# A two-layer feed-forward stage whose TensorE and ScalarE instructions are put in the program's order

## The chip, the cores and the metric

The kernel runs on one core of one Trainium2 chip, as one launch. The metric is the device time of that launch in microseconds (us). TensorE is called PE in the profile (its weight loads PEld), VectorE DVE, ScalarE ACT, GpSimd POOL; SP only issues DMAs.

## The reference

Eight sublayers run one after another on 2048 tokens of width 128. The change is in the sixth, "L2 feed-forward" (`l2f`), which is itself two layers of local attention followed by a gated MLP. Cut to what matters:

```python
def _layer(x, wqkv, qs, ksc, wo, lg, lb, w1, b1, w2, b2):
    h = shift_token(x)                       # half of the channels from the token before
    q, k, v = split(h @ wqkv)                # 8 heads of 64
    q = l2norm(q) * qs ; k = l2norm(k) * ksc
    q, k = rotary_xpos(q, k)
    o = local_attention(q, k, v)             # window 64: own window and the one before
    x = x + o @ wo
    h = layernorm(shift_token(x)) * lg + lb
    a, g = split(h @ w1 + b1)                # 341 + 341
    return x + (a * gelu(g)) @ w2 + b2
```

After the two layers, `l2f` adds its own input and normalizes again. All of it is float32.

## The kernel before, in words

`l2f` works on tiles of 128 tokens (16 a layer, so T = 32 tiles in all) and on blocks of four tiles (512 tokens, four a layer). A software pipeline runs over **ticks**; at one tick several functions run, each for another tile. For tile t:

- `project(t)`, at tick t: two matmuls of 512 columns give q and k into a PSUM tile `p`; ScalarE squares it into `sq` (L1095), VectorE sums the squares per head into `rn` (L1099), multiplies `p` by the rotary tables into `qk` (L1108) and, in two halves, into the reused `sq` (L1110, L1111), and GpSimd adds the two (L1113). At each odd tick ScalarE takes the root of `rn` for two tiles (L1102), GpSimd clips it (L1103), VectorE inverts it (L1104), and GpSimd scales `qk` of both tiles (L1118). A third matmul gives v, which ScalarE copies out (L1122).
- `turn(t)`, at tick t+2: eight transposes of `qk`, then ScalarE copies `qT` (L1139) and `kT` (L1140), and GpSimd takes the 64 columns before from the last `kT` (L1144).
- `probs(t)`, at tick t+3: two bf16 matmuls add the mask (L1153, the "band"), 32 small ones the scores (L1165) into the PSUM tile `s`; VectorE takes the maxima `em` (L1173), ScalarE makes eight exponentials (L1178), VectorE inverts the sums `den` (L1185) and GpSimd scales `e` (L1186).
- `turn_probs(t)`, at tick t+4: eight transposes of `e` (L1194), which VectorE copies to `et` (L1196).
- `mixed(t)`, at tick t+4: 32 small matmuls of `et` with v into `po` (L1211); ScalarE copies `po` into the block's `oT` (L1218).
- `ff1` to `ff7`, for a whole block, one a tick: output projection and residual; shift and layer norm; the transposes back; the first MLP matrix with gelu (`ff4`: three pairs of matmuls in `p2` tiles, L1263, gelu L1266, product L1269); the second matrix (`ff5`); the last norm (`ff6`, `ff7`, second layer only). `forward(tick, odd)` calls those that are due. Piece k is due when `tick - 8 - k` is a multiple of four.

So four ticks make a period. I call them by their piece: **A** (tick a multiple of 4: `ff1`, and `ff5` of the block before), **B** (`ff2`, and `ff6` in the second layer), **C** (`ff3`, `ff7`), **D** (`ff4`).

[...] The pool `p2` holds three tiles of two banks, shared in turn by `s`, `p`, the transposes of `turn` and `turn_probs`, and the three accumulators of `ff4`. The pool `ps_t` holds two tiles of one bank (`tp`), shared by v's product, `po`, and every accumulator and transpose of the pieces except `ff4`'s.

The order in which an engine takes its instructions is set when the program is built: a scheduler takes what it reckons ready first, by priorities that follow the program, and picks the buffer of each tile. Each engine then works through its own list in that order, and waits on semaphores. The order of the tick's calls is

```python
for tick in range(T + 11):
    due = lambda lag: 0 <= tick - lag < T
    forward(tick, True)      # ff5, ff6, ff7
    if due(3): probs(tick - 3)
    if due(0): project(tick)
    forward(tick, False)     # ff1 .. ff4
    if due(4): turn_probs(tick - 4)
    if due(2): turn(tick - 2)
    if due(4): mixed(tick - 4)
```

The activation tables of Sqrt, Exp and Gelu are loaded separately (ACT_TABLE_LOAD in the profile).

## Time and profile before

| | |
|---|---|
| runs | 2861.51, 2861.67, 2853.43 us; median 2861.51 |
| profiled execution | 2845.6 us, span 2843.8 us |
| mean granted TensorE clock | 0.949 |
| busy, share of the span | PE 90%, PEld 57%, DVE 58%, ACT 52%, POOL 22% |
| `l2f`, first projection to the first matmul of the next stage | 824.07 to 1273.13 us |

The median of the runs is 15.9 us (0.56%) above the profiled execution, and the runs lie within 8.2 us of each other. Windows below are microseconds from the start of the span.

### The profile page before, as it was taken

What the parts mean: (1) busy time and instruction counts of PE and PEld (TensorE: products, weight loads), DVE (VectorE), ACT (ScalarE), POOL (GpSimd) and SP (SyncE); (2) the same over time, 40 slices, a digit from 0 to 9 for tenths busy, and PEclk for the clock granted to TensorE, in tenths of its full rate; (3) what the DMA queues carried; (4) which work ended last, traced back from release to release, by engine and by line L of the source; (5) the groups of instructions that cost most, each with busy time, mean ns of one, the idle gap of its engine ahead of it and who ended that gap; (6) DMA issues with size and microseconds to landing.
All of it is one profiled execution on the core that took longest, in us unless ns stands there. A gap on an engine that the chain in (4) does not pass through costs nothing.

```text
span 2843.8 us, 59514 instructions
## 1 busy us (share of the span) xinstructions
PE 2564.7 (90%) x24826; PEld 1608.3 (57%) x24826; DVE 1650.6 (58%) x2624; ACT 1474.9 (52%) x2968; POOL 632.4 (22%) x773
## 2 busy tenths in 40 slices
PE   5789569988878888879999999999999999999998
PEld 3456334432225444436777767777677776777543
DVE  6443242116676566546777767777677776777411
ACT  1113212234537666536676666666567665766422
POOL 2142341015568666520000000000000000000000
PEclk9679868989989999989999999999999999999999
DMA  3101100000011111010000000000000000000000
GB/s 142 56 22 37 32 13 6 0 23 8 8 51 40 27 31 53 19 41 13 10 6 9 9 6 9 9 6 9 9 6 9 9 6 9 6 9 6 1 8 8
DMA packets 30930, 55.59 MB, mean 20 GB/s; under 512 B 5388, under 2 KB 18644, under 8 KB 29380
## 3 DMA queue, kind: packets, MB, share of 16 engines
q1 hardware_dynamic: 27958, 45.09, 5.5%
q0 software_dynamic: 2272, 4.66, 0.7%
q8 instruction: 198, 3.24, 0.5%
q10 hardware_dynamic: 432, 2.04, 0.2%
q14 instruction: 70, 0.57, 0.1%
HBM read 29.49 MB, written 4.71 MB: 12 GB/s over the span
## 4 chain that ended last, share of the span: by engine, by line
PE 77%; DVE 12%; POOL 4%; ACT 3%; issue 2%; DMA 1%; SPq 0%; POOLq 0%; DVEq 0%; ACTq 0%
PE po L1438 17%; PE s L1399 16%; PE t L1423 10%; PE mm L834 8%; PE h L645 2%; DVE h L980 2%; PE tp L675 1%; PE tp L1476 1%; PE tp L1379 1%; PE p L1087 1%; PE p L1263 1%; PE mm L823 1%; PE tp L1501 1%; DVE ln_xn L276 1%; PE mm L845 1%
## 5 line engine op out<-in xcount | busy, mean ns | idle before, releaser
L1413 ACT ACTIVATE e<-s,nm 128x1024 f32<-128x1024 f32 x512 | 574.2, 1121 | 395.5 <-DVE nm L1407 395.5
L1407 DVE TENSOR_REDUCE nm<-s 128x1 f32<-128x1024 f32 x512 | 602.6, 1219 | 40.4 <-PE s L1399 40.2
L1438 PE MATMUL po<-et,v 128*64 128x128 f32 x8192 | 505.6, 276 | 0.0
L1399 PE MATMUL s<-kT,qT 64*128 64x512 f32 x1024 | 495.0, 603 | 1.2 <-ACT e L1413 1.2
L1399 PE MATMUL s<-kT,qx 64*128 64x512 f32 x1024 | 494.9, 603 | 0.0
L1425 DVE COPY et<-t 128x512 f32<-128x512 f32 x512 | 350.8, 685 | 211.0 <-ACT et L1426 93.0
L1438 PEld LDWEIGHTS po<-et,v 128*64 128x64 f32 x8192 | 443.5, 137 | 17.5 <-issue 0.2
L1423 PEld LDWEIGHTS t<-con,e 64*128 64x128 f32 x8192 | 319.8, 139 | 207.8 <-issue 109.1
L1423 PE MATMUL t<-con,e 64*128 64x64 f32 x8192 | 358.0, 226 | 2.9 <-ACT e L1413 1.7
L1426 ACT COPY et<-t 128x512 f32<-128x512 f32 x512 | 301.3, 588 | 49.3 <-PE t L1423 49.1
L1457 POOL TENSOR_TENSOR f<-m,nm 128x8 f32<-128x8 f32 x64 | 12.9, 202 | 1117.9 <-DVE m L1455 1117.9
L834 PE MATMUL mm<-h,w 128*128 128x512 f32 x512 | 221.1, 592 | 0.1
L1399 PEld LDWEIGHTS s<-kT,qT 64*128 64x128 f32 x1024 | 173.3, 189 | 62.4 <-issue 51.8
L1399 PEld LDWEIGHTS s<-kT,qx 64*128 64x128 f32 x1024 | 173.3, 188 | 59.3 <-ACT e L1413 31.1
L834 PEld LDWEIGHTS mm<-h,w 128*128 128x128 f32 x512 | 97.2, 190 | 122.3 <-issue 119.4
L847 DVE SCALAR_TENSOR_TENSOR r<-mm,vec,xT 128x512 f32<-128x512 f32 x8 | 6.0, 751 | 239.8 <-PE mm L845 239.8
L841 ACT ACTIVATE h<-mm,vec 128x512 f32<-128x512 f32 x64 | 44.0, 687 | 157.3 <-PE mm L834 157.2
L1178 ACT ACTIVATE e<-p,em 128x128 f32<-128x128 f32 x256 | 90.5, 381 | 40.6 <-DVE em L1173 38.6
L272 POOL TENSOR_SCALAR ln_rs<-ln_mv 128x4 f32<-128x4 f32 x40 | 10.5, 264 | 425.3 <-DVE ln_mv L270 387.2
L1413 ACT ACTIVATION_READ_ACCUMULATOR e<-s,nm 128x1 f32 x512 | 102.7, 201 | 0.0
L284 PE MATMUL tp<-con,ln_xn 128*128 128x128 f32 x144 | 33.0, 336 | 64.2 <-DVE ln_xn L276 64.2
L986 POOL TENSOR_TENSOR hc<-h,bc 128x1024 f32<-128x1024 f32 x32 | 75.2, 2351 | 63.9 <-DVE h L980 53.9
(340 smaller groups left out, 3782.1 us busy)
## 6 DMA issues: line engine op xcount, KB each, us to landing
qx<-qT SPq DMA_DIRECT2D x64, 128.0 KB, 2.2
vo<-v SPq DMA_DIRECT2D x62, 128.0 KB, 2.2
ex<-in_w_ex_dram SPq DMA_DIRECT2D x4, 1536.0 KB, 14.2
rot<-in_rot_dram SPq DMA_DIRECT2D x32, 128.0 KB, 2.3
w<-in_w_l2f_dram SPq DMA_DIRECT2D x2, 1557.0 KB
w<-in_w_l1f_dram SPq DMA_DIRECT2D x1, 2816.0 KB, 9.7
w<-in_w_l3f_dram SPq DMA_DIRECT2D x1, 2816.0 KB
yd<-ys SPq DMA_DIRECT2D x39, 64.0 KB, 1.5
```

Of the source, the lines that this page charges most:

```text
L645: nc.tensor.matmul(h[:, i], lhsT=xt, rhs=self.ex[:, bass.ds(e, 1), i * 512 : (i + 1) * 512].rearrange("p a b -> p (a b)"), start=False, st ...
L834: nc.tensor.matmul(p, lhsT=hid[i][:, k, c * 128 : (c + 1) * 128], rhs=h[:, k, :], start=k == 0, stop=k == 3,)
L980: nc.vector.tensor_tensor_scan(h[:, i], dA[:, i], pu[:, i], carry_of[b - 1][:, g : g + 1], ALU.mult, ALU.add)
L986: nc.gpsimd.tensor_mul(hc, h, bc[:, 1].unsqueeze(1).to_broadcast([128, 2, TB]))
L1178: nc.scalar.activation(e[:, r, c, :], s[:, r, c, :], AF.Exp, bias=m[:, r, c : c + 1], accum_out=den[:, r, c : c + 1],)
L1399: nc.tensor.matmul(p[:, i, :], lhsT=q_of[b, 4 * g + h][i][r, t * 128 : (t + 1) * 128], rhs=kT[r, g, c * 512 : (c + 1) * 512], start=True, ...
L1407: nc.vector.tensor_reduce(nm_of[k][:, h, c : c + 1], p, AX.X, ALU.max, negate=True)
L1413: nc.scalar.activation(e, p, AF.Exp, bias=nm_of[k][:, h, c : c + 1], accum_out=den_of[k][:, h, c : c + 1])
L1423: nc.tensor.transpose(tp[i][:, j, :], e[r, j * 128 : (j + 1) * 128], self.ident[r, r])
L1425: nc.vector.tensor_copy(et[:, 0], tp[0])
L1426: nc.scalar.copy(et[:, 1], tp[1])
L1438: nc.tensor.matmul(po_of[k][r, h, :].rearrange("p (i q) -> p i q", i=2), lhsT=v[:, t, g * 64 : (g + 1) * 64], rhs=ets[c][:, :, j, :], star ...
```

## The change

It is in `l2f` alone. (1) A `manual_schedule` block over PE and Activation makes those two engines take their instructions in the order in which the program states them; VectorE, GpSimd and SP stay with the scheduler. (2) `mixed` runs at tick t+5 in place of t+4, between `project` and the pieces. (3) The root and what follows it leave `project` and become `norms`, called at the end of each odd tick behind the pieces. (4) All pieces run at one place, behind `mixed`, in reversed order (`ff7` first). (5) VectorE copies `po` out in place of ScalarE. (6) `v` and `vo` have six buffers in place of five.

```diff
                 nc.vector.tensor_reduce(rn[:, t % 2], ...)
-                if t % 2:
-                    nc.scalar.activation(rn, rn, AF.Sqrt)
-                    nc.gpsimd.tensor_scalar(rn, rn, 1e-12, None, ALU.max)
-                    nc.vector.reciprocal(rn, rn)
...
-                if t % 2:
-                    for i in (0, 1):
-                        g = qk_of[t - 1 + i].rearrange("p (g d) -> p g d", d=64)
-                        nc.gpsimd.tensor_mul(g, g, rn[:, i].unsqueeze(2).to_broadcast([128, 16, 64]))
...
-                v = self.tile(sb, [128, 512], "v", bufs=5)
+                v = self.tile(sb, [128, 512], "v", bufs=6)
-                vo = self.tile(sb, [128, 512], "vo", bufs=5)
+                vo = self.tile(sb, [128, 512], "vo", bufs=6)
...
+            def norms(t):
+                rn = rn_of.pop(t // 2)
+                nc.scalar.activation(rn, rn, AF.Sqrt)
+                nc.gpsimd.tensor_scalar(rn, rn, 1e-12, None, ALU.max)
+                nc.vector.reciprocal(rn, rn)
+                for i in (0, 1):
+                    g = qk_of[t - 1 + i].rearrange("p (g d) -> p g d", d=64)
+                    nc.gpsimd.tensor_mul(g, g, rn[:, i].unsqueeze(2).to_broadcast([128, 16, 64]))
...
-                nc.scalar.copy(o_of[n, b][:, :, j * 128 : (j + 1) * 128], po)
+                nc.vector.tensor_copy(o_of[n, b][:, :, j * 128 : (j + 1) * 128], po)
...
-            def forward(tick, odd):
-                for k, piece in enumerate(pieces):
+            def forward(tick):
+                for k, piece in reversed(list(enumerate(pieces))):
                     vb, rest = divmod(tick - 8 - k, 4)
-                    if rest == 0 and 0 <= vb < T // 4 and (k >= 4) == odd:
+                    if rest == 0 and 0 <= vb < T // 4:
                         piece(*divmod(vb, NB))

-            for tick in range(T + 11):
-                due = lambda lag: 0 <= tick - lag < T
-                forward(tick, True)
-                if due(3):
-                    probs(tick - 3)
-                if due(0):
-                    project(tick)
-                forward(tick, False)
-                if due(4):
-                    turn_probs(tick - 4)
-                if due(2):
-                    turn(tick - 2)
-                if due(4):
-                    mixed(tick - 4)
+            with self.tc.manual_schedule(engines={mybir.EngineType.PE, mybir.EngineType.Activation}):
+                for tick in range(T + 11):
+                    due = lambda lag: 0 <= tick - lag < T
+                    if due(3):
+                        probs(tick - 3)
+                    if due(0):
+                        project(tick)
+                    if due(5):
+                        mixed(tick - 5)
+                    forward(tick)
+                    if due(0) and tick % 2:
+                        norms(tick)
+                    if due(4):
+                        turn_probs(tick - 4)
+                    if due(2):
+                        turn(tick - 2)
```

## The prediction

> **What bounds the kernel now.** Sections 1 and 2 of the page first: PE is the busiest engine; in `l2f`, the 12th to the 18th of the 40 slices, its digit is 7 or 8, behind it 9, so there is something to win and to lose. The windows view then gives one steady period of four ticks:

> ```profile
> PE 2564.7 (90%) x24826; PEld 1608.3 (57%) x24826; DVE 1650.6 (58%) x2624; ACT 1474.9 (52%) x2968; POOL 632.4 (22%) x773
> ...
> PE   5789569988878888879999999999999999999998
> ```

> ```profile
> core 0: us, PE busy (x) PEld busy (x) DVE busy (x) ACT busy (x) POOL busy (x), PEclk, DMA share, GB/s
> 1045.38:1096.70 51.32, 42.44 (x387) 24.93 (x388) 31.01 (x48) 33.76 (x95) 32.95 (x30) 1.00 0.13 33
> ```

> No engine is full: PE idles some 9 of 51.3 us at full clock, the others 17 to 20. The period is set by chains from engine to engine. The timelines of VectorE and PE show the longest, in tick D (from `em` to the second half of `sq`, on which the third pair of `ff4` waits), and what ends ticks A and B:

> ```profile
> 1077.39 1.23 DVE L1173 TENSOR_REDUCE em<-p 128x8 f32<-128x1024 f32 x1 [2.25 <-PE p L1165]
> 1082.56 1.22 DVE L1099 TENSOR_REDUCE rn<-sq 128x16 f32<-128x1024 f32 x1 [0.71 <-ACT sq L1095]
> 1083.70 1.21 DVE L1108 TENSOR_TENSOR qk<-p,rot 128x1024 f32<-128x1024 f32 x1
> 1085.43 0.68 DVE L1111 TENSOR_TENSOR sq<-p,rot 128x512 f32<-128x512 f32 x1
> ...
> 1086.26 1.92 PE L1263 MATMUL p<-hn,w 128*85 128x512 f32 x4 [2.60 <-DVE sq L1111]
> 1105.80 0.59 PE L1153 MATMUL p<-band,ident_b 128*128 128x512 bf16 x2 [1.22 <-ACT kT L1140]
> 1115.19 0.59 PE L1153 MATMUL p<-band,ident_b 128*128 128x512 bf16 x2 [1.27 <-ACT kT L1140]
> ```

> From `em` to the end of `sq` 8.72 us pass. The score matmuls (L1165) start at 1076.22, 1095.53, 1106.33, 1115.71 and 1127.54, so before, D takes 19.31 us, A 10.80, B 9.38, C 11.83: 51.32.

> The waits view (860 to 1240) shows what the change aims at, and the groups view what it moves:

> ```profile
> PEld tp L1211 <- DVE et L1196: 22.0, 19, 4.1
> PE p L1263 <- DVE sq L1111: 15.6, 6, 2.6
> PE tp L1211 <- DVE et L1196: 10.5, 14, 3.8
> L1218 ACT COPY oT<-tp 128x512 f32<-128x512 f32 x12 | 7.0, 585 | 4.5 <-PE tp L1211 4.5
> L1266 ACT ACT_TABLE_LOAD x6 | 7.7, 1283 | 0.1
> ```

> **The change part by part.** The order in the built program shows that it does as it says: PE and ScalarE stand in the program's order. So each tick can be laid end to end from rows of before. The rows, start to next start: `project` 1.75 after the scores end, v 0.86, `mixed` 1.09, `turn_probs` and `turn` 1.04 each, band 0.53, scores 1.10, `ff1` 3.44, `ff5` 2.77, a pair of `ff4` 1.72, `ff2` or `ff3` 0.44; an engine starts 0.07 to 0.1 after the one it waits for.

> *Mixed a tick later.* `et` is then a tick old; PE's 10.5 us on it go (PEld's 22.0 lie mostly under matmuls). *Copy by VectorE.* No row has this copy on VectorE; the same shape out of PSUM, in the next stage (L1425), has a mean of 685 ns, 660 to 693, against ScalarE's 585: 32 copies, 22 us more on VectorE, 19 less on ScalarE. What counts is who waits. `po` and v hold the two `tp` banks, and in the built program the piece in A, B and C takes `po`'s: `mixed` ends 3.77 after the scores, the copy ends 4.53, the piece starts 4.60 in place of 3.70. New PE idle: 0.9 in three ticks of four; behind the waiting piece stand both transposes, so ScalarE's `kT` and the next scores wait with it. VectorE queues the copy right behind `em`, so nothing else holds it. [...] Left on ScalarE in program order the copy would stand behind eight exponentials (2.76, from 1099.30 to 1102.06), which is far worse.

> *Roots at the tick's end.* Gelu no longer alternates with Sqrt: the built program has 7 Gelu loads for 13, so 6 x 1.283 = 7.7 us of ScalarE go. After a load the next activation starts at once (load 1085.03 + 1.28, root 1086.32). [...] It does cost: `turn`'s copies now stand behind root and load, and the Exp load of ticks A and C waits for `em`. Before, C's ran under it (load 1069.14, `em` ended 1069.74).

> *v and vo's sixth buffer* keeps v for the later `mixed`; the DMAs and their 2.2 us landing lie a tick ahead: nothing.

> **The four ticks, from scores' end to scores' end.**
> A: `ff5` 4.60 to 7.37, `ff1` to 10.81 (its bank, v's, is free at 7.0: `em` 1.31, load to 2.66, exponentials 2.76, `sq` 0.9, v 0.63), both transposes to 12.89, `kT` copied by 14.1 (0.09+0.48+0.59), scores to **15.25**.
> B: transposes done at 7.1; but the band's `p2` tile is the last `p`, free after the 8.72 chain, at 9.0 (it starts 0.08 late, and a norm statistic stands in it). Band 9.15, scores to **10.78**.
> C: VectorE has `ln_xn` ahead of `em`, `ln_xn` waits for GpSimd's `ln_rs`, and in the new order that stands behind the addition of B's `qk`:

> ```profile
> 1115.14 0.23 POOL L272 TENSOR_SCALAR ln_rs<-ln_mv 128x4 f32<-128x4 f32 x1
> 1115.45 1.04 POOL L273 TENSOR_TENSOR ln_rs<-ln_rs,mhalf 128x4 f32<-128x4 f32 x1
> 1116.44 0.40 POOL L1144 COPY kT<-kT 128x256 f32<-128x256 f32 x1
> ...
> 1117.36 2.35 POOL L1113 TENSOR_TENSOR qk<-qk,sq 128x1024 f32<-128x1024 f32 x1
> ```

> In B's time: addition 9.1 to 11.4, `kT` piece 0.36, `ln_rs` to 13.2, `ln_xn` to 14.4; so `em` of C starts 3.6 after its scores. Load to 6.2, exponentials to 9.05; `turn` takes the tile they read: to 10.15; ScalarE is through `sq` and v at 10.4, `kT` 11.45, scores to **12.6**.
> D: VectorE is still on C's `sq` until 13.54, so `em` is 0.93 late; chain to 9.65, third pair 9.75 to 11.47, its gelu to 12.4, load and root to 13.9, copies to 15.0, scores to **16.16**.
> Sum 54.79, against 51.32: **+3.5 us a period**. D gains 3.15, since `mixed` and `ff5` leave it, A loses 4.45, C 0.8, B 1.4: PE does the same matmuls, but idles 13 us, not 9.

> The stage, by the same laying: ticks 3 to 7, without pieces, take 46.3 (9.5 where the root and its load, done 7.2 after the scores, stand ahead of `kT` and scores; 8.5 and 9.3 in the even ones) for the 50.6 between `em` at 843.02 and 893.62, but the first `em` comes 2.7 later (both tiles' sums before the first root, and the next projection behind the last stage's transposes): -1.6. Ticks 8 to 11, A without `ff5` (12.5): 52.0 for 48.88, +3.1. Ticks 12 to 27, four periods: +13.9. Ticks 28 to 31, where `ff6` puts a second `ln_rs` and `ln_xn` ahead of C's `em` (7.0 late, C 18.9, D then 15.3): 60.2 for 58.14, +2.0. Tick 32, with `mixed` and `ff5` now behind the scores: 11.7 for 8.9, +2.8; behind it the two are level. Sum **+20.2 us**: 2845.6 would become 2866 in a profiled execution, and the median 2861.5 becomes 2881.5 (0.7%). Hand-overs are the softest term: 0.05 us more or less at six a tick over 29 ticks is 9 us each way, and the copy's bounds under 1 us; so this case alone spans 2871 to 2893.

> **Rivals.** *Faster.* The two new holds do not bind: `po` is free before a piece needs it (0.9 x 3 = 2.7 a period), and `em` of C is not held by `ln_rs` (3.6). Then a period is 48.5, and over the six of ticks 8 to 31 the 20.2 turn into -17.6: 2844. It decides from 4.8 of these 6.3 us on (20.2 + 8.6 = 6 x 4.8). For it: the wait of `mixed` on `et` is removed, and ScalarE is freed of 27 us (19 + 7.7). Against: both holds follow from single queues as built.
> *No change.* Only C's hold is absent: 51.2 a period, 20.2 - 6 x 3.6 = -1.4: 2860. Against: before, C's `em` also started late behind `ln_xn` (1119.84, scores ended 1116.81: 3.0).
> *Slower still.* ScalarE's fixed order costs more than I laid: where `turn`'s copies wait for the root, or v for late exponentials, by a further 0.6 us a tick: +17, 2898.
> *It does nothing*: excluded by the order.

> **How the numbers follow.** A measurement here can tell 0.3% (8.6 us) from no change. My case 0.65, nearly all above +8.6; slower still 0.10; no change 0.11; faster 0.14. So faster 0.14, same 0.11, slower 0.75. The range 2855 to 2896 leaves out most of the faster case and half of the slowest.

> **What would show it.** Right: PE's waits of `mixed` on `et` gone; a wait of `ff1`, `ff2`, `ff3`, `ff5` on VectorE's `oT` of some 0.8 us; A near 15 us, D near 16, the period near 54.8; Exp loads that wait for `em` in A and C. Wrong: `em` of C directly behind its scores, or a period under 51.

## The result, and the profile after

| | before | after |
|---|---|---|
| runs, us | 2853.43 to 2861.67, median 2860.28 (4 runs) | 2894.24 to 2899.93, median 2898.18 (4 runs) |
| ratio, 95% interval | | 1.0139 [1.0122, 1.0157] |
| profiled execution, span | 2843.8 us | 2892.2 us |
| `l2f`, first projection to the first matmul of the next stage | 449.1 us | 486.8 us |

The change made the kernel slower by 37.9 us. I had said slower by 20.2, with a range up to 2896: the direction was right, the size about half, and the median lies 2.2 us above the range. The stage alone is 37.7 us longer, which is the whole of it; the two profiled executions differ by 12.5 us more ahead of the stage, where nothing was edited (the last section says what that is).

First the page after, sections 1 and 2: PE's busy time, its digits, and the granted clock.

```profile
PE 2586.8 (89%) x24826; PEld 1619.9 (56%) x24826; DVE 1674.5 (58%) x2656; ACT 1447.7 (50%) x2930; POOL 632.3 (22%) x773
...
PE   5789569988867787778999999999999999999998
...
PEclk8579868989889999898999999999999999999999
```

PE has the same 24826 matmuls and is busy 22 us longer: 11.6 of them in the stage and 12.0 ahead of it, with 1.5 less behind it. The same work takes longer. The PEclk row all but hides why: a mean clock of 0.94 prints as 9, as 1.00 does, and only the windows below tell them apart.

The stage cut at the start of `em` of the ticks (the em of tick t is that of tile t-3). "Half" counts the stretches of 3.41 us in which the trace grants half the clock:

| part | before, us (half) | after, us (half) | change | forecast |
|---|---|---|---|---|
| first projection to first em (tick 3) | 18.96 (2) | 23.48 (3) | +4.5 | +2.7 |
| ticks 3 to 8 | 50.59 (3) | 48.66 (1) | -1.9 | -4.3 |
| ticks 8 to 12 | 48.88 (0) | 53.99 (2) | +5.1 | +3.1 |
| ticks 12 to 28 | 205.54 (0) | 223.26 (6) | +17.7 | +13.9 |
| ticks 28 to 32 | 58.13 (1) | 62.40 (4) | +4.3 | +2.0 |
| tick 32 to the next stage | 66.96 (5) | 74.97 (7) | +8.0 | +2.8 |

Two periods of the steady part, from the windows view of the kernel after:

```profile
core 0: us, PE busy (x) PEld busy (x) DVE busy (x) ACT busy (x) POOL busy (x), PEclk, DMA share, GB/s
1018.81:1074.76 55.95, 45.22 (x387) 26.62 (x388) 34.30 (x52) 30.11 (x90) 33.01 (x30) 0.94 0.12 29
1074.76:1129.69 54.93, 42.03 (x387) 24.89 (x388) 34.30 (x53) 30.10 (x90) 33.02 (x30) 1.00 0.12 30
```

The second has the full clock and takes 54.93 us; the forecast's four ticks added up to 54.79. The first does the same at a mean clock of 0.94 and takes 1.02 more: PE is busy 3.2 us longer for the same matmuls. Inside the second, the timelines of the engines show the holds that were forecast:

```profile
1079.36 2.84 PE L1282 MATMUL tp<-f,w 128*128 128x512 f32 x6 [0.79 <-DVE oT L1219]
1099.00 0.61 PE L1154 MATMUL p<-band,ident_b 128*128 128x512 bf16 x2 [2.09 <-DVE sq L1106]
1103.20 1.37 DVE L276 TENSOR_SCALAR ln_xn<-tp,ln_mv,ln_rs 128x128 f32<-128x128 f32 x4 [2.06 <-POOL ln_rs L273]
1104.48 1.21 DVE L1174 TENSOR_REDUCE em<-p 128x8 f32<-128x1024 f32 x1
1105.77 1.28 ACT L1179 ACT_TABLE_LOAD   x1 [7.70 <-DVE em L1174]
```

`ff5` waits 0.79 us for the copy of `po`; the band of B waits for the last `sq` of the chain of `p`; in C VectorE stands at `ln_xn` for `ln_rs`, and `em`, whose scores ended at 1100.64, starts 3.8 us late with the Exp load behind it. So the steady part's order was read rightly, and something else was left out.

### The profile page after: what moved, and what is told of

Read it like the earlier page. It is cut to its first block, busy times and chain, and to the rows that moved or that the text cites. A ratio compares the mean times of both kernels' runs of the same rounds, so it can differ in the third digit from the quotient of the medians.

```text
span 2892.2 us, 59530 instructions
## 1 busy us (share of the span) xinstructions
PE 2586.8 (89%) x24826; PEld 1619.9 (56%) x24826; DVE 1674.5 (58%) x2656; ACT 1447.7 (50%) x2930; POOL 632.3 (22%) x773
## 4 chain that ended last, share of the span: by engine, by line
PE 78%; DVE 10%; ACT 5%; POOL 3%; issue 2%; DMA 1%; SPq 0%; POOLq 0%; DVEq 0%; ACTq 0%
PE po L1441 17%; PE s L1402 15%; PE t L1426 10%; PE mm L834 8%; PE h L645 2%; DVE h L980 2%; PE p L1087 1%; PE tp L675 1%; PE tp L1479 1%; PE p L1264 1%; ACT e L1179 1%; PE tp L1382 1%; POOL ln_rs L273 1%; DVE ln_xn L276 1%; PE tp L886 1%
## 5 line engine op out<-in xcount | busy, mean ns | idle before, releaser
L1441 PEld LDWEIGHTS po<-et,v 128*64 128x64 f32 x8192 | 443.5, 137 | 17.5 <-issue 0.2
L272 POOL TENSOR_SCALAR ln_rs<-ln_mv 128x4 f32<-128x4 f32 x40 | 10.5, 262 | 429.6 <-DVE ln_mv L270 391.4
L284 PE MATMUL tp<-con,ln_xn 128*128 128x128 f32 x144 | 33.8, 346 | 72.9 <-DVE ln_xn L276 64.2
## 6 DMA issues: line engine op xcount, KB each, us to landing
ex<-in_w_ex_dram SPq DMA_DIRECT2D x4, 1536.0 KB, 14.1
```

Source lines behind the costliest of these rows:

```text
L1441: nc.tensor.matmul(po_of[k][r, h, :].rearrange("p (i q) -> p i q", i=2), lhsT=v[:, t, g * 64 : (g + 1) * 64], rhs=ets[c][:, :, j, :], star ...
```

## What was left out: the clock

```profile
1036.62:1040.04 3.42, 2.54 (x46) 2.43 (x47) 1.59 (x4) 3.40 (x13) 1.35 (x1) 1.00 0.00 0
1040.04:1043.45 3.41, 1.32 (x11) 0.79 (x9) 3.41 (x7) 2.07 (x4) 1.64 (x5) 1.00 0.33 77
1043.45:1046.86 3.41, 3.41 (x35) 2.36 (x35) 1.73 (x7) 0.00 (x0) 3.24 (x4) 0.50 0.13 38
...
1094.65:1098.06 3.41, 2.26 (x20) 2.02 (x19) 2.86 (x4) 3.38 (x6) 2.27 (x3) 1.00 0.34 77
1098.06:1101.48 3.42, 2.48 (x36) 1.46 (x37) 3.08 (x11) 0.01 (x1) 2.45 (x2) 1.00 0.14 41
```

and PE's timeline of the same two places:

```profile
1043.05 0.68 PE L1154 MATMUL p<-band,ident_b 128*128 128x512 bf16 x2 [2.09 <-DVE sq L1106]
1043.65 1.99 PE L1166 MATMUL p<-kT,qT 64*64 64x128 f32 x32
...
1099.54 1.10 PE L1166 MATMUL p<-kT,qT 64*64 64x128 f32 x32
```

The wait is 2.09 us both times. In the first period it lies within one stretch (1040.04 to 1043.45), PE is busy for 1.32 of 3.41 us (0.39), and the next stretch is granted 0.50: the scores take 1.99 us for 1.10. In the second an edge of the grid (1098.06) cuts the wait in two, both stretches are busy for 0.66 or more, and the one behind them (1101.48 to 1104.89) is granted 1.00. I laid all 20 kernels of this study on the grid, ticks 8 to 32: after 1770 stretches at full clock the next was at half 83 times. Of those 83, 78 came after a stretch in which PE was busy for less than 0.42; of the 1687 that were followed by full clock, 3 were. In before and after alone, the 8 drops of these ticks came behind stretches busy for 0.20 to 0.41, and the other 168 were busy for 0.43 or more. The count speaks for these ticks: ahead of the stage, the execution of before also has a drop behind a stretch that was busy for 0.93 (794.36 to 797.77). A period of 54.93 us is 16.09 stretches, so the gaps move over the grid from one period to the next: of the four periods of ticks 12 to 28, three have half-clock stretches (56.13, 55.95 and 56.25 us at a mean clock of 0.94) and one has none (54.93 at 1.00).

The kernel before has such a wait too: 2.60 us of PE in every D, longer than those. But its period of 51.33 us is 15.04 stretches, so it nearly stands still on the grid, and in the profiled execution an edge cut that wait in all six D's of ticks 8 to 32. Laid elsewhere, one stretch could hold the whole wait and be busy for 0.24 of it (2.60 of 3.41 us idle). That the 0 in ticks 8 to 28 before is in part a matter of where this execution lay on the grid is my estimate from that and the count above; no run shows the kernel at another place. The run mix1 below is a like case: a period of 51.18 us (14.99 stretches), a wait of some 3.45 us ahead of B's band in each of the four periods of ticks 12 to 28 (17.5 us in five such waits over 860 to 1250), and no stretch at half clock in them.

## The experiments

Verdicts use ratios to the kernel before, run on the same chip (95% intervals). Executions of one kernel spread over as much as 26 us (l_st, 2840.15 to 2866.55), and the profiled ones differ by up to 19 us ahead of the stage, so the stage's own times in the profiled executions, one for each kernel, are shown beside them. The medians come from several chips, on which the kernel before took from 2851.22 (beside copy, b_copy, sched and b_lag) to 2860.28 us, so an expected median is best read with the ratio beside it. "12-28" is the time of ticks 12 to 28, "end" that from em of tick 32 to the next stage, half-clock stretches in brackets.

| label | median, us | ratio | stage, us | start | 12-28 | end |
|---|---|---|---|---|---|---|
| before | 2860.28 | | 449.1 | 18.96 (2) | 205.54 (0) | 66.96 (5) |
| after | 2898.18 | 1.0139 [1.0122, 1.0157] | 486.8 | 23.48 (3) | 223.26 (6) | 74.97 (7) |
| fill | 2887.61 | 1.0109 [1.0085, 1.0133] | 483.1 | 22.20 (3) | 219.34 (0) | 73.38 (4) |
| ff2 | 2877.49 | 1.0078 [1.0050, 1.0105] | 469.8 | 23.49 (3) | 214.96 (5) | 74.77 (6) |
| early | 2880.80 | 1.0076 [1.0049, 1.0103] | 472.7 | 22.22 (3) | 211.12 (2) | 70.63 (5) |
| tail | 2891.18 | 1.0110 [1.0083, 1.0137] | 485.6 | 22.21 (3) | 223.37 (6) | 71.45 (5) |
| copy | 2938.71 | 1.0303 [1.0280, 1.0326] | 533.5 | 22.20 (3) | 250.94 (15) | 84.07 (10) |
| b_copy | 2892.30 | 1.0139 [1.0117, 1.0162] | 480.9 | 16.53 (0) | 238.78 (11) | 67.02 (5) |
| sched | 2855.99 | 1.0011 [0.9992, 1.0031] | 454.7 | 20.13 (1) | 208.28 (5) | 70.10 (4) |
| b_lag | 2861.52 | 1.0037 [1.0018, 1.0056] | 458.9 | 16.58 (0) | 218.40 (9) | 65.63 (5) |
| s_ff2 | 2866.90 | 1.0043 [1.0029, 1.0058] | 461.7 | 22.80 (3) | 216.87 (5) | 70.83 (6) |
| b_ff2 | 2858.21 | 1.0008 [0.9994, 1.0022] | 452.2 | 19.32 (2) | 207.79 (3) | 67.74 (5) |
| mix1 | 2874.34 | 1.0067 [1.0043, 1.0090] | 461.8 | 22.22 (3) | 204.74 (0) | 75.08 (7) |
| last | 2853.62 | 1.0005 [0.9991, 1.0019] | 451.6 | 22.21 (3) | 202.82 (0) | 72.88 (6) |
| l_s | 2854.10 | 1.0004 [0.9985, 1.0023] | 448.1 | 19.59 (2) | 202.81 (0) | 72.90 (6) |
| l_t | 2851.19 | 0.9983 [0.9970, 0.9996] | 448.7 | 22.17 (3) | 202.70 (0) | 67.40 (5) |
| l_st | 2852.02 | 0.9989 [0.9971, 1.0006] | 449.0 | 22.07 (3) | 202.84 (0) | 67.88 (6) |
| l_fill | 2859.27 | 1.0020 [1.0006, 1.0033] | 454.8 | 22.19 (3) | 202.60 (0) | 76.33 (4) |
| l_t2 | 2860.69 | 1.0010 [0.9993, 1.0027] | 451.7 | 22.18 (3) | 202.68 (0) | 73.19 (6) |
| l_t3 | 2856.54 | 1.0008 [0.9991, 1.0025] | 449.3 | 23.48 (3) | 202.62 (0) | 72.79 (6) |

**fill: does the clock cost, or only go along?** Unused matmuls in the three long gaps of a period.

```diff
+            def filler():
+                z = self.tile(self.ps_t, [128, 512], "tp")
+                for _ in range(4):
+                    nc.tensor.matmul(z, lhsT=ident_b, rhs=bands[0]..., start=True, stop=True)
# called ahead of ff4's third pair; in C ahead of turn; in B behind turn
```

> The changed kernel with work added: four bf16 matmuls of 512 columns (about 1.0 us together at full clock), whose result nobody reads, in each of three gaps of TensorE in a period: ahead of the third pair of ff4 in D (idle 2.25 us after), behind turn in B (2.09) and between the transposes of e and of qk in C (2.02). Theory 'clock': what my forecast left out is the granted clock, which falls to 0.50 for one or more stretches of 3.41 us after a stretch in which TensorE was busy for less than about 0.43; fuller gaps then keep the clock up: ticks 12 to 28 at a mean clock of 0.99 or 1.00 in place of 0.95, 219 to 220 us in place of 223.3, although the program does more, and the whole 2886 to 2893. Rival 'order': the excess lies in waits of the fixed order, and the low clock goes with them without costing anything; then nothing is gained and the fillers may cost up to 1 us each: 2897 to 2915.

The windows view of fill, two periods:

```profile
1067.45:1122.37 54.92, 44.39 (x395) 26.06 (x400) 34.29 (x52) 30.10 (x90) 33.10 (x30) 1.00 0.12 30
1122.37:1177.28 54.91, 44.38 (x395) 26.05 (x400) 34.28 (x52) 30.10 (x90) 33.16 (x30) 1.00 0.19 54
```

PE does more, and all four periods run at full clock in 54.58 to 54.93 us: 223.26 becomes 219.34. Added dead work shortens this part by 3.9 us, so the low clock was a cost of its own and its removal leaves the forecast's period. It is not only a lucky place on the grid: if a window of 3.41 us is slid over fill's four periods, the least busy place is still 0.41 to 0.48 busy, against 0.34 in the full-clock period of the kernel after. Outside the steady part the fillers won nothing (ticks 8 to 12 kept their 2 half-clock stretches, ticks 28 to 32 took 63.57 us), so that the stage is 3.7 us shorter; the medians say 10.6, with intervals that meet.

**ff2 and early: the hold of C.** ff2 calls ff2 and ff6 between `probs` and `project`; early calls `mixed` first in the tick besides.

```diff
+                    forward(tick, (1, 5))          # ff2, ff6
                     if due(0):
                         project(tick)
                     if due(5):
                         mixed(tick - 5)
-                    forward(tick)
+                    forward(tick, (0, 2, 3, 4, 6))
```

> The changed kernel with ff2 (and ff6) called between probs and project in place of behind mixed, so that GpSimd has ln_rs ahead of the addition of B's qk. The forecast's own step: em of C is no longer 3.6 to 3.8 us late behind ln_xn, so a period at full clock goes from 54.9 to 51.3 or a little more, six periods save some 20 us, 2876 to 2880. Theory 'clock' adds that it may go 6 us either way, as gaps move against the 3.41 us stretches. Rival: the hold only hid what is late next (turn of C waits for the exponentials, then for the chain in D), and the period falls by under 1.5 us: 2889 to 2898.

> As the kernel with ff2 ahead of project, and mixed called first in the tick, ahead of probs, so that TensorE does it while ScalarE copies kT, and no piece waits for the copy of po. Forecast's steps: A falls by the 0.9 of the copy and the 1.09 of mixed, B and C stay on the chain of p (10.8), D 15.2: a period of 50.0 to 50.5 and six of them 26 to 29 us under the changed kernel: 2868 to 2873. Theory 'clock': mixed fills the gap ahead of the scores, clock near 1.00 in ticks 12 to 28, and so another 6 us off: 2863 to 2869. Rival: et, made just before, holds mixed and with it the scores, as in the kernel before, so that A gains nothing: 2876 or more.

GpSimd in B, first the kernel after, then that of ff2 (timelines); in the second `ln_rs` is done before the addition:

```profile
1099.03 2.36 POOL L1108 TENSOR_TENSOR qk<-qk,sq 128x1024 f32<-128x1024 f32 x1 [1.57 <-DVE sq L1106]
1101.82 0.23 POOL L272 TENSOR_SCALAR ln_rs<-ln_mv 128x4 f32<-128x4 f32 x1
```

```profile
1134.10 1.04 POOL L273 TENSOR_TENSOR ln_rs<-ln_rs,mhalf 128x4 f32<-128x4 f32 x1
1140.14 2.35 POOL L1108 TENSOR_TENSOR qk<-qk,sq 128x1024 f32<-128x1024 f32 x1 [1.13 <-DVE sq L1106]
```

`em` of C then follows its scores at once, and the period at full clock goes from 54.93 to 51.93 (forecast 51.3); the median is 2877.49, in the stated 2876 to 2880. Where half-clock stretches fall, ff2's periods are 53.29 to 54.88. early took A only from 15.09 to 14.86: `et`, transposed just before, holds `mixed` in front of the scores (PE waits 13.8 us for it over 860 to 1250). D grew to 16.25. That is its rival, though ticks 12 to 28 had 2 half-clock stretches for 5.

**sched, b_lag, b_copy, copy: which edit costs.** sched takes away the `manual_schedule` block alone. b_lag and b_copy give the kernel before one edit each, `mixed` at t+5 behind `project` with six buffers, or the copy on VectorE. copy puts the copy back on ScalarE in the fixed order.

```diff
-            with self.tc.manual_schedule(engines={...PE, ...Activation}):     # sched
+            if True:
-                nc.scalar.copy(o_of[n, b][...], po)                           # b_copy; copy is the reverse, on the kernel after
+                nc.vector.tensor_copy(o_of[n, b][...], po)
```

> The changed kernel without the manual_schedule block: lag, copy, roots, pieces and buffers are as changed, and the scheduler orders TensorE and ScalarE. In the built program it puts the next tick's mixed into the wait for kT. Theory: the loss is that of the fixed order (piece behind the copy, C's em behind ln_xn, gaps long enough to lower the clock), so that the period is 51 or less and the whole 2850 to 2864. Rival: the loss comes with the moved steps themselves (lag, copy on VectorE, roots late, pieces together): 2880 to 2898.

> The kernel before with mixed a tick later, called behind project, and six buffers for v and vo; all else, the scheduler too, as before. Theory: TensorE's waits on et (10.5 us on PE in 860 to 1240) go and A is shorter by up to 1 us, but the chain of p in B and D sets the ends of three ticks: 2852 to 2862. Rival: mixed later holds the oT of ff1 back in A (ff1 needs the copy of the same tick, which ScalarE does behind the exponentials): 2865 to 2875.

> The kernel before with nothing changed but the copy of po, which VectorE does (22 us more on VectorE, 19 less on ScalarE); the scheduler places everything. Forecast's step taken alone: 0.1 us a copy, and where VectorE's chain in D takes the copy in, 0.7 a period: 2860 to 2866. Rival: the copy holds po's bank behind VectorE's queue as in the changed kernel, 0.9 in three ticks of four, 2.7 a period: 2876 to 2880.

> The changed kernel with the copy of po back on ScalarE, still in the program's order. Forecast's step: the copy then stands behind load, exponentials, square and v (9.0 us after the scores in A and C, where mixed ends at 3.8), and the piece that takes po's bank starts at about 9.1 in place of 4.6: +4.4 in A, +3 to 4 in B and C, some 11 us a period; about 2950 to 2970. Rival: the exponentials are late anyway and the piece has slack, so the copy's place costs what it did on VectorE: 2895 to 2905.

Without the fixed order the change costs nothing that can be measured (1.0011, the interval includes 1), though its periods take 51.6 to 53.0 us, over the 51 expected, and its profiled stage is 5.6 us longer than before. PE in sched, tick D to A (timeline): the scheduler puts part of the next `mixed` and half of the next projection between the band and the scores. ScalarE's copy of `kT` runs from 1103.94 to 1104.53, so PE goes on working past it.

```profile
1103.98 0.38 PE L1154 MATMUL p<-band,ident_b 128*128 128x512 bf16 x1 [0.61 <-DVE et L1197]
1104.50 0.34 PE L1212 MATMUL tp<-et,vo 128*64 128x64 f32 x4
1104.66 0.29 PE L1212 MATMUL tp<-et,v 128*64 128x64 f32 x4
1104.88 1.12 PE L1087 MATMUL p<-w,hT 128*128 128x512 f32 x2
1105.94 1.10 PE L1166 MATMUL p<-kT,qT 64*64 64x128 f32 x32
```

b_copy was a miss on both sides: 1.0139, 2892.30, above its rival's 2880. The copy's own 0.1 us cannot make that. In its built order the scheduler puts `ln_rs` behind both scalings of `qk` too, so the same hold of C grows (timelines of GpSimd and VectorE):

```profile
1097.36 2.35 POOL L1113 TENSOR_TENSOR qk<-qk,sq 128x1024 f32<-128x1024 f32 x1
1099.67 3.76 POOL L1118 TENSOR_TENSOR qk<-qk,rn 128x1024 f32<-128x1024 f32 x2
1103.51 0.23 POOL L272 TENSOR_SCALAR ln_rs<-ln_mv 128x4 f32<-128x4 f32 x1
...
1105.46 1.37 DVE L276 TENSOR_SCALAR ln_xn<-tp,ln_mv,ln_rs 128x128 f32<-128x128 f32 x4 [6.59 <-POOL ln_rs L273]
```

`em` of B to `em` of C takes 18.79 us there, for 11.77 before: 28 of the 33.2 us that ticks 12 to 28 lost; 11 half-clock stretches go with the rest. In b_lag the waits of `mixed` on `et` are gone (0.5 us over 860 to 1250, for 10.5 on PE and 22.0 on PEld before), yet A is longer, 12.24 for 11.37, and the whole slower by 0.4%: inside its theory's 2852 to 2862 by the number, not by the reason. In copy, A grows from 15.09 to between 17.44 and 20.43 and C by 3.9, but B not at all: 2938.71, under the 2950 expected (by its ratio it would be 2947 where before takes 2860) and far from the rival.

**mix1: the hold of the copy.** On ff2, `mixed` goes ahead of `project`.

```diff
+                    if due(5):
+                        mixed(tick - 5)
                     forward(tick, (1, 5))
                     if due(0):
                         project(tick)
-                    if due(5):
-                        mixed(tick - 5)
```

> The kernel of the run ff2 (fixed order, ff2 early) with mixed called ahead of project in place of behind it, so that the copy of po has the time of p's and v's matmuls (2.6 us), and no piece should wait for it. Forecast's step: the 0.9 us goes in A alone, since B and C are set by the chain of p and by the exponentials: the period at full clock 51.9 to 51.0, six of them 5 us: 2870 to 2874. Rival: p stands 1.09 us later and with it its chain, which sets B and D: +2 a period, 2885 or more. Rival two: the 0.9 counts in three ticks, -2.7 a period: 2860 to 2865.

PE's waits on `oT` fall from 9.6 us (ff2, 860 to 1250) to 1.8, the period from 51.93 to 51.18: the sum is as forecast, its place is not. A loses 0.22, B gains 0.30, and C loses 0.83 (10.75 to 9.92): the term binds in C, where `ff3` stood behind the copy. The edit moves the matmuls of `mixed` too, so 0.75 is a net figure.

**s_ff2, b_ff2: the same hold under the scheduler.** The same early ff2 and ff6, on sched and on the kernel before.

> The kernel of the run sched (all of the change but the fixed order) with ff2 and ff6 called between probs and project. Theory: the hold of C's em behind ln_rs and ln_xn, worth 3.0 us a period in the fixed order (54.93 to 51.93), is there in the scheduler's order too, in part (ln_xn waits 9.3 us for ln_rs over 860 to 1250, 1 us a time); without it a period falls by 1 to 3 us from 51.8: 2842 to 2852. Rival: the scheduler had already put other work over that hold, and the statistics in front of rn delay the chain of p in B: 2856 to 2870.

> The kernel before with ff2 and ff6 called between probs and project, nothing else. Theory: C's em, 3.0 late behind ln_xn before, comes right behind its scores, and the period falls from 51.3 to 49 or so: 2838 to 2850. Rival: what is late next is the chain of p, and the norm's transposes ahead of p delay it: 2860 to 2875.

Neither theory held: early statistics gain nothing (b_ff2 1.0008, between its two ranges), and s_ff2 lies at 1.0043, in its rival's range, for sched's 1.0011, with one half-clock stretch or more in every period. What B gains is lost elsewhere: in s_ff2 B falls from 13.2 to 9.4 and A grows from 12.46 to 17.56; in b_ff2 B falls by 0.8, and C and D grow by 0.8 and 0.3.

**last: another fixed order.** On ff2, the other pieces go behind `turn`.

```diff
-                    forward(tick, (0, 2, 3, 4, 6))
...
                     if due(2):
                         turn(tick - 2)
+                    forward(tick, (0, 2, 3, 4, 6))
```

> The kernel of the run ff2 with the other pieces called behind turn, at the end of the tick, so that they stand in the wait for kT's copy and no transpose stands behind a piece that waits. Forecast's way of laying: A 13.75 (scores need no wait behind ff1), B 10.8, C 10.8 to 12, D 13 to 15, a period of 49 to 51 and fewer gaps, hence fewer half-clock stretches: 2860 to 2872. Rival: ff4's tiles stand in front of the next band, and its gelu behind kT's copy lengthens D to 17 or more: 2880 to 2895.

The windows view of last:

```profile
1063.85:1114.56 50.71, 41.43 (x383) 24.60 (x388) 34.09 (x52) 30.07 (x90) 32.80 (x30) 1.00 0.13 32
```

Every steady period is 50.7 us, with no half-clock stretch from tick 12 to 32: faster there than before by 2.7 us. A took 14.21, B 11.83, C 10.62 and D 14.06, near what was laid; the median, 2853.62, is better than the 2860 to 2872 expected, by its ratio (1.0005) inside it. So a fixed order as such is no loss; the one of the change was.

**tail and the l_ runs: the two ends.** tail is the kernel after, the l_ runs are last, with another order at an end.

```diff
+            for tick in range(0, 3): one(tick)              # scheduler; l_s, l_st
             with self.tc.manual_schedule(...):
-                for tick in range(T + 11):
+                for tick in range(3, T): one(tick)          # l_st; l_s from 3 to T + 11; l_t and tail from 0 to T
+            for tick in range(T, T + 11): end(tick)         # scheduler; l_t, l_st: calls of before, mixed at t+4; tail: as changed
# l_t2, l_t3: the same from T + 3 on; l_t3 with the last transposes of e and mixed ahead of the pieces
# l_fill: last with eight unused bf16 matmuls of 512 columns behind the pieces from tick 36 on
```

> The changed kernel with the program's order kept for ticks 0 to 31 alone; from tick 32 on the scheduler places the instructions of TensorE and ScalarE. Theory 'clock' for the end: of the 8.0 us that the end of the stage lost, most is the fixed order (mixed and transposes ahead of ff4) and the half clock that its gaps bring; ticks 32 to the end fall from 75.0 to 67 or 69, and the whole to 2889 to 2892. Rival: the end is a chain that has the same length in either order, and the later root and mixed lengthen it: 74 to 76, 2897 to 2899.

> The kernel of the run last with the program's order on TensorE and ScalarE from tick 3 on alone; ticks 0 to 2 are left to the scheduler. Theory: the start's loss is the fixed order (the stage before still has transposes and copies to do, and v of the first tile stands ahead of project of the second): from the first projection to the first em 19 to 20 us in place of 22.2, the whole 2850 to 2852. Rival: the start is the later root and the same in either order, 22 to 23 us, 2853 to 2856.

> The kernel of the run last with the program's order for ticks 0 to 31, and from tick 32 on the scheduler, with the calls in the order of the kernel before and mixed at t+4 again. Theory: the end's loss is the order and the extra tick of mixed: from em of tick 32 to the next stage 67 to 68 us in place of 72.9, the whole 2848 to 2850. Rival: the end is set by the clock and the last block's chain, 71 to 73 us, 2852 to 2855.

> Both of these together, so that the program's order holds in ticks 3 to 31 alone. Theory: the two gains add up: start 19 to 20, end 67 to 68, the whole 2844 to 2848, under the kernel before (2855.8) by 8 to 12 us. Rival: what is won at one end moves into the ticks behind it: 2851 to 2856.

> The kernel of the run last with work added whose result nobody reads: eight bf16 matmuls of 512 columns (some 2 us) behind the pieces of each tick from tick 36 on, where TensorE waits for the last block's chain. Theory 'clock' for the end: TensorE then does more than 0.43 of most 3.41 us stretches, the 6 half-clock stretches of the end become 3 or fewer, ff4 of the last block runs in 6 us, and the end takes 69 to 71 us in place of 72.9: 2850 to 2852. Rival: the fillers hold up the chain or the chain is not TensorE's, so that the end takes 72 to 76 us: 2853 to 2857.

> As l_t, but the program's order holds through tick 34, and the scheduler takes over at tick 35, with the calls of the kernel before (pieces, then the last transposes of e and mixed). Theory: ticks 28 to 32 take 52.8 again and the end 67 to 69: 2847 to 2850. Rival: the end's gain needs the scheduler in ticks 32 to 34 as well, 71 to 73 us: 2851 to 2855.

> As l_t2 with the last transposes of e and mixed called ahead of tick 35's pieces, so that the last block's chain starts before ff4 of the block before. Theory: the end is the last block's chain behind the last mixed, so ff1 starts some 5 us earlier and the end takes 64 to 67 us: 2844 to 2848. Rival: ff4 and ff5 of the block before then stand in the chain's gaps in single-buffered tiles and hold it as long: 67 to 72 us.

The end. The last `ff1` (L1227 before, L1228 after) starts the last block's chain. PE's timelines of before, after and l_t:

```profile
1228.33 1.98 PE L1263 MATMUL p<-hn,w 128*128 128x512 f32 x4 [0.60 <-DVE hn L1244]
1230.25 0.34 PE L1211 MATMUL tp<-et,vo 128*64 128x64 f32 x4
...
1231.33 3.70 PE L1263 MATMUL p<-hn,w 128*128 128x512 f32 x8
1234.87 1.04 PE L1194 MATMUL p<-con,e 128*128 128x128 f32 x8
1241.48 3.60 PE L1227 MATMUL tp<-oT,w 128*128 128x512 f32 x8
```

```profile
1275.15 0.48 PE L1212 MATMUL tp<-et,vo 128*64 128x64 f32 x4 [1.32 <-DVE et L1197]
1277.05 6.35 PE L1264 MATMUL p<-hn,w 128*128 128x512 f32 x12
1283.24 1.04 PE L1195 MATMUL p<-con,e 128*128 128x128 f32 x8
1289.86 3.60 PE L1228 MATMUL tp<-oT,w 128*128 128x512 f32 x8
```

```profile
1241.28 1.04 PE L1195 MATMUL p<-con,e 128*128 128x128 f32 x8
1247.89 3.60 PE L1228 MATMUL tp<-oT,w 128*128 128x512 f32 x8
```

From em of tick 32 (1206.17, 1248.34, 1212.51) that is 35.3, 41.5 and 35.4 us. Of the 8.0 us, 6.2 arise ahead of it; 2.8 of them were forecast, since `mixed` and `ff5` of tick 32 now stand behind its scores. `ff4` of the block before, with the last transposes of `e` behind it in both kernels, starts 28.7 us after that em in place of 22.2: in the fixed order it stands behind `mixed`, which waits for `et` and runs at half clock, where the scheduler had put `mixed` between its pairs. tail, which changes nothing but who orders these ticks, has the last `ff1` at 38.8 us and gives 3.5 of the 8.0 back (71.45, under the 74 of its rival and over the 69 of its theory, with 5 half-clock stretches for 7; the median, 2891.18, lies in the theory's range). No run separates the clock from the order in that.

l_t has an end of 67.40 for last's 72.88, but took 55.53 for 52.80 in ticks 28 to 32, where `ff5` and a second `mixed` again stand ahead of the scores of tick 32: 2.8 us are left of the 5.5. From em of tick 28 to the next stage it takes 122.9 us, last 125.7, before 125.1. l_t2 (126.0) and l_t3 (125.6) gain nothing, so the place is ticks 32 to 34, not the last ones; l_t3 fits neither of its ranges for the end. l_fill brought the half-clock stretches from 6 to 4 and made the end longer, 76.33: its last `ff4` ran in 5.3 us for 8.0 in last, but started 3.5 later, and the fillers stand between the pieces ahead of it.

The start. l_s and l_st give PE the same order there, but took 19.59 and 22.07 us, with 2 and 3 half-clock stretches, the second with half clock at its beginning; all fixed-order starts are 22.2 to 23.5 with 3, the others 16.5 (0) to 22.8 (3). How much of the start is order and how much the grid stays open; the theory of l_s (19 to 20) held in l_s and failed in l_st, and the medians (1.0004, 0.9989) show no gain.

l_t is a little faster than the kernel before: 2851.19 against 2855.84 us, 0.9983 [0.9970, 0.9996]. With 19 kernels compared and a stage of 448.7 for 449.1 us, that is a hint rather than a gain shown. l_st adds nothing to it that can be told (0.9989 [0.9971, 1.0006]).

## Why the prediction was off

*The four ticks.* Right. At full clock em to em takes 15.09 (A), 14.63, 9.90 and 15.31 after; the steps gave 15.25, 14.4 (10.78 plus C's late 3.6), 9.9 and 15.2. 54.93 for 54.79.

*The two holds.* Both bind. C's is worth 3.0 us a period (ff2; forecast 3.6). The copy's is worth 0.75 net (mix1), a good quarter of the 2.7 that the rival "faster" put on it, and in C, not in the A where the sum had it. *The copy on ScalarE far worse*: shown, by a ratio of 1.0303 for 1.0139 and 47 us of the stage.

*Cover at nothing.* Gelu loads, lag and buffers: no gain seen; and no run shows a gain from the waits on `et`, the change's aim (sched 1.0011, b_lag 1.0037), though the kernel after has none of them left ahead of `mixed` over 860 to 1250. The signs that the prediction named, those waits gone, 0.8 us on `oT`, the Exp load waiting for `em`, all came.

*The failing step* is the sentence "each tick can be laid end to end from rows of before" where it gives the time of the stage: the sum has the granted clock at nothing, without a reason. All those rows were taken at full clock, and I laid 13 us of idle in place of 9 without asking what that does to the clock. With fill as measure it is 3.9 us of ticks 12 to 28, where 17.7 = 13.9 + 3.9 leaves nothing over. The profile of before had the evidence: 11 half-clock stretches towards both ends of the stage, where TensorE has long gaps (the stage's eight drops came behind stretches busy for 0.37 or less). And my own sum put the band of B (free at 9.1, transposes done at 7.1) and the third pair of D behind such gaps: the trace of after has them at 2.09 and 2.25 us. In ticks 8 to 12 (+5.1 for +3.1) it shows again: D took 16.95 us there in place of 15.31, and in ff2, with the same A (12.51) and no half-clock stretch, D took 15.31; that is 1.6 of the 2.0.

*The second step that failed*, and the largest single miss, is "behind it the two are level", said of what follows tick 32: +2.8 for the 8.0 that the end lost. I laid tick 32 alone, while the last `ff1` came 6.2 us later. 3.5 of the missing 5.2 come back when the scheduler orders these ticks (tail); the rest is open, and so is how much of it is clock.

The sum missed 17.5 us in all: 5.2 at the end, 3.8 in ticks 12 to 28, 2.0 in ticks 8 to 12, 2.3 in ticks 28 to 32 (+4.3 for +2.0, with 4 half-clock stretches), and 4.2 ahead of tick 8 (ticks 3 to 8, -4.3 for -1.9, and the start, +2.7 for +4.5). The last two go with half-clock stretches, but no run separated clock from order there. Had either failed step been laid rightly, the median would have lain inside the range. My rival "slower still" had the size, 2898, by a mechanism (ScalarE's order, 0.6 a tick) that the steady periods do not show: its number is luck.

## What to carry to other kernels

Lay the ticks of a fixed order end to end from rows of the trace: that gave the period within 0.15 us. Then mark the long waits of TensorE (2.02 to 2.60 us here) and look at the clock that was granted behind each: in the kernel after the same wait of 2.09 us was followed by 0.50 in one period and by 1.00 in the next, and the half clock was worth 3.9 us of ticks 12 to 28 (fill). A period near a whole number of stretches (15.04 before, 14.99 in mix1) keeps its place on the grid, and both profiles show such waits without half clock in ticks 12 to 28; that they need not be free elsewhere on the grid is my estimate. And lay out the fill and drain of a pipeline as carefully as its period. A hold on a shared queue (here `ln_rs` on GpSimd) was worth 3.0 us a period in the kernel after, 7.0 more than before in b_copy, and nothing in all under the scheduler's order of before (b_ff2), depending on where one instruction stands, so compare queues before blaming the instruction that was moved.

## What I had not expected of the hardware

How short a gap went with half clock: in ticks 8 to 32 of these 20 kernels, 78 of the 81 stretches of 3.41 us at full clock in which PE was busy for less than 0.42 were followed by one at half, though over a whole period of the kernel after PE is busy for 0.77 (42.03 of 54.93 us). And the spread between executions goes with the half clock too. In the 20 profiled executions the stage starts between 821.1 and 840.0 us, though no edit lies ahead of it, and the trace counts 67 half-clock stretches ahead of it in the earliest and 80 in the latest (69 in before, 77 in after; correlation 0.97): about 1.3 us for each by a straight line through all 20. What follows the stage took 1568.4 to 1571.1 us in all of them. Among the runs of one kernel, too, the time follows the mean granted clock: the correlation is -0.92 to -1.00 in each of the 11 changed kernels with ten runs or more. Two kernels are therefore better compared by their stage than by a few medians, but a stage's time is that of one execution too: its start took 16.5 us with no half-clock stretch and 22.1 to 23.5 with three.
